# Routing and the first expert of a mixture layer: three groups of instructions in another order

## The chip, the cores and the metric

The kernel runs on one core of a Trainium2 chip. The metric is the device time of one launch in microseconds (us), the median of three runs. Beside the runs there is one profiled execution, whose trace gives the start and the length of each instruction on each engine: TensorE (PE, with its weight loads as PEld), VectorE (DVE), ScalarE (ACT), GpSimd (POOL) and SyncE (SP), which here only issues DMAs.

## The reference

Four layers on x of 8 x 256 rows of 512, each added to x: an attention with a decay mask, a feed-forward of ternary weights, an attention with gates (mLSTM), and a mixture of experts. The change lies at the border between the third and the fourth. The fourth is, cut to what matters:

```python
def _moe_core(x, gate_w, w13, w2):            # x: 2048 rows of 512, E = 32 experts, K = 4
    N = T * K
    C = 2 * N // E
    logits = jnp.einsum('th,eh->te', x, gate_w)
    scores = jax.nn.softmax(logits, axis=-1)
    topk_w, topk_ids = jax.lax.top_k(scores, K)
    topk_w = topk_w / jnp.sum(topk_w, axis=-1, keepdims=True)
    ...
    buf = jnp.zeros((E, C, x.shape[1]), x.dtype).at[sorted_eid, pos].set(x[tok], mode='drop')
    gu = jnp.einsum('ech,ehf->ecf', buf, w13)
    g, u = jnp.split(gu, 2, axis=-1)
    eo = jnp.einsum('eci,eih->ech', jax.nn.silu(g) * u, w2)
    out_slots = eo[sorted_eid, pos]
    return jnp.zeros_like(x).at[tok].add(out_slots * flat_w[order][:, None])

h = _rmsnorm(hidden_states, norm_w)
routed = _moe_core(x, gate_w, w13, w2)
shared = jax.nn.silu(x @ shared_gate_w) * (x @ shared_up_w) @ shared_down_w
out = residual + (routed + shared)
```

So each row goes through a shared expert and through the four experts of its own.

## The kernel before

**Stages.** Rows are kept as 16 tiles of 128, and, turned, as four chunks of 512 columns (`g.qT`). The first two layers and the gated attention take the first 520 us. Around 520 us the last normalized rows are turned, the logits are computed (`logits`, `logits_turned`), and `choices` finds each row's four experts, the rank of each expert by the number of its rows, and each row's place in its expert's list. `route` turns these into lists: which row stands in which slot of which rank (`g.tok_of`), and to which row a slot's result is added (`g.to`). Then the 32 experts run in the order of their ranks (`layer1_ffn`), from about 600 us to the end.

**The shared expert** fills TensorE beside all this. Its chunks 0 and 1 (`EARLY = 2`) are cut into pieces that `filler()` puts between the steps of the attention's last rounds and of `choices`. A piece is a pair: matmuls, and what follows on them (`rest`), which waits in the list `then` for the next call. For the last first-product piece of chunk 1, `rest` is `gated(1)`: a silu on ScalarE (L1068) and a product on VectorE (L1069) that gives `act`, which the second products (`down`, L1080) of chunk 1 read. Each `yield` of `choices` is one call of `filler()`. Up to here the order of TensorE, ScalarE, VectorE, GpSimd and SyncE is that of the program (`manual_schedule`).

Chunks 2 and 3 are done by `glu` and `down` in `layer1_ffn` (L1775 to L1781). `glu` writes four products of a chunk (pg and pu for two halves of the hidden width, L1744) into three PSUM buffers (`gu`), a silu frees the buffer of pg, the product L1749 on VectorE frees that of pu and gives `act`. `down` (L1761) has two buffers (`po`) and reads both halves of `act`; VectorE adds its result to the row (L1780) and SP writes the row out (L1781). A product of f32 shows in the trace as two instructions for each matmul of the code, so a chunk is 32 instructions of L1744 and 16 of L1761.

**Order in the free stretch.** From `route` to the last shared product no order is written out. The framework's scheduler makes it when the program is built: it steps through the program with its own estimates of durations, and gives each engine that falls free the first instruction in program order that is ready by these estimates. On the chip each engine then keeps that order, ready or not. `route` stands ahead of chunks 2 and 3 in the program, so its work goes first where it is ready, and the shared work fills in.

**The lists.** `route` builds them in eight passes (`n`, two for each of a row's four places). A pass compares the list numbers of eight row tiles with the numbers 0 to 127 of all lists (`to_list`, L1645, two buffers), and then for each tile makes a matrix of slot numbers (`to_slot`, L1651, four buffers) whose product with the tile's part of `to_list` is added up in one PSUM buffer (`pl`, L1654). So there are 64 slots and 64 list products. Ahead of the passes stand constants: three iotas on GpSimd (`iota`, `iop`, `lists_i`), their casts on VectorE, and the comparisons that give `g.is_rank` and `g.expert` (L1629 to L1637); `spare` is read only after the passes (L1666), `g.expert` by the load of an expert's weights on SP (L1724). After the passes: `tok_of` (L1663), and the check whether an expert has too many rows (`limit`, `g.over`; L1672 to L1682), which the code has last in `route`.

Before `route`, `layer1_ffn` fills a tile with zeros on GpSimd and writes it from GpSimd's queue to the 512 rows behind the output (L1768 to L1770), to which the empty slots add.

**The first expert.** `fetch` gathers a block of up to 128 rows from memory by `tok_of` (an indirect DMA on GpSimd's queue, six buffers). `turn_block(r, j)` turns block j of rank r: four transposes on TensorE (pt, L1801, two buffers), a product with the norm's weights on VectorE (xT, L1802), the slots' weights (`of`, L1796), and it issues the gather of block j of rank r + 2. From L1831 on the order of TensorE, ScalarE and VectorE is written out again; it begins with the four turns of rank 0.

```python
        with tc.manual_schedule(engines={E_.PE, E_.Activation, E_.DVE}):
            for j in range(NJ):
                turn_block(0, j)
            for r in range(E):
                w13, w2 = load_expert(r)
                act = glu(ps, w13[:, :, :FI], w13[:, :, FI:], xT.pop(r), SLOTS[r], partial(turn_block, r + 1))
```

## Time and profile before

| What | us |
|---|---|
| runs: median (lowest to highest) | 1031.09 (1029.36 to 1031.83) |
| the profiled execution | 1030.34 |
| its span in the trace | 1028.6 |
| last shared pieces of chunk 1 done (TensorE) | 547.2 |
| first list product | 554.6 |
| last list product | 582.6 |
| first gather issued on GpSimd | 584.3 |
| first turn of rank 0 | 595.95 |
| first product of rank 0 | 599.44 |

The times below the span are starts or ends in the trace, counted from the span's start. An engine's busy time in a window of the trace says how full it is there; the idle time that the trace notes in front of an instruction, with the instruction that ended it, says for what it waited.

### The profile page before, as it was taken

The page shows a single profiled execution, that of the slowest core. Times are in us where ns is not written, and L with a number is a line of the kernel's source. Part 1 is how long each engine was busy: PE and PEld are TensorE (multiplying, and loading weights), DVE is VectorE, ACT ScalarE, POOL GpSimd, SP SyncE. Part 2 cuts the span into 40 slices and gives each one's busy share as a digit, 9 for nine tenths or more (in the row PEclk, how much of TensorE's full clock was granted, in tenths as well). Part 3 has the DMA queues.
Part 4 walks back from the last instruction along what each step waited for, and adds up shares of the span by engine and source line. Part 5 has one row for each costly group of instructions (what it writes and reads, how often), then busy time and mean ns, then how long its engine had stood idle before and what let it go on. Part 6 is the DMA issues. An engine that isn't in the chain of part 4 may idle for free.

```text
span 1028.6 us, 14755 instructions
## 1 busy us (share of the span) xinstructions
PE 990.8 (96%) x5220; PEld 603.4 (59%) x5220; DVE 527.2 (51%) x1338; ACT 404.1 (39%) x693; POOL 404.5 (39%) x501
## 2 busy tenths in 40 slices
PE   8999999989999899999999999999999999999995
PEld 6766656534444356666544445555666666778783
DVE  7446566679987858878969831211212221122110
ACT  4443343457776757877430002122122222221221
POOL 0023443430111113788303225455455555444432
PEclk9999999999999999999999999999999999999998
DMA  9853333324332511231116248687788788889983
GB/s 344 294 185 117 141 118 130 103 67 76 60 58 40 92 39 45 64 126 55 62 62 225 82 147 189 169 209 190 182 207 207 207 210 231 220 242 240 230 225 46
DMA packets 101154, 152.67 MB, mean 148 GB/s; under 512 B 39592, under 2 KB 42280, under 8 KB 101036
## 3 DMA queue, kind: packets, MB, share of 16 engines
q1 hardware_dynamic: 82128, 107.04, 34.1%
q0 software_dynamic: 18944, 44.60, 19.4%
q8 instruction: 43, 0.70, 0.3%
q14 instruction: 39, 0.32, 0.1%
HBM read 110.42 MB, written 33.23 MB: 140 GB/s over the span
## 4 chain that ended last, share of the span: by engine, by line
PE 72%; DVE 13%; DMA 4%; POOL 4%; ACT 3%; issue 2%; SPq 0%; POOLq 0%; ACTq 0%; DVEq 0%
PE po L1761 14%; PE pg L1744 13%; PE pu L1744 13%; PE pw L399 5%; PE pz L435 5%; PE pt L1801 3%; PE p L1203 2%; DMA wst<-in_w1T 2%; DVE am L1220 2%; PE pgu L1060 2%; DVE h L1216 2%; DVE ct L844 2%; PE po L415 1%; PE po L412 1%; DVE st L127 1%
## 5 line engine op out<-in xcount | busy, mean ns | idle before, releaser
L1749 DVE TENSOR_TENSOR act<-pu,sg 128x264 f32<-128x264 f32 (+22 forms) x68 | 31.9, 469 | 313.5 <-PE pu L1744 303.2
L1786 POOL DMA_INDIRECT xg<-h_d,tok_of x85 | 83.6, 983 | 196.0 <-DVE of L1796 64.1
L1805 POOL DMA_INDIRECT out_x<-eo,to x85 | 132.9, 1564 | 55.1 <-ACT eo L1843 34.3
L1761 PE MATMUL po<-w,act 128*128 128x512 f32 (+10 forms) x456 | 143.1, 489 | 0.0
L1744 PE MATMUL pg<-xT,w 128*128 128x216 f32 (+21 forms) x512 | 134.9, 406 | 0.7 <-DVE xT L1802 0.7
L1843 ACT ACTIVATE eo<-po,slotw 128x512 f32<-128x512 f32 (+10 forms) x114 | 65.1, 576 | 173.9 <-PE po L1761 166.9
L1744 PE MATMUL pu<-xT,w 128*128 128x216 f32 (+21 forms) x512 | 133.3, 403 | 0.0
L1744 PEld LDWEIGHTS pg<-xT,w 128*128 128x128 f32 x512 | 93.2, 190 | 33.2 <-issue 16.9
L1748 ACT ACTIVATE sg<-pg 128x264 f32<-128x264 f32 (+22 forms) x68 | 28.5, 420 | 213.5 <-PE pg L1744 213.5
L1744 PEld LDWEIGHTS pu<-xT,w 128*128 128x128 f32 x512 | 96.8, 190 | 26.2 <-issue 5.6
L1203 PE MATMUL p<-wq,xqT 128*128 128x512 bf16 (+1 forms) x384 | 82.9, 367 | 6.4 <-DVE qi L1224 3.1
L1761 PEld LDWEIGHTS po<-w,act 128*128 128x128 f32 (+10 forms) x456 | 54.1, 155 | 57.5 <-issue 47.6
L420 POOL TENSOR_TENSOR y<-y,gam 128x512 f32<-128x512 f32 x16 | 20.2, 1265 | 135.5 <-DVE y L81 135.5
L1203 PEld LDWEIGHTS <-xqT 128*128 128x128 bf16 x384 | 37.6, 99 | 50.2 <-issue 13.6
L1802 DVE TENSOR_TENSOR xT<-pt,nw 128x512 f32<-128x512 f32 (+12 forms) x85 | 51.1, 601 | 20.5 <-PE pt L1801 20.5
L435 PE MATMUL pz<-wo,wyT 128*128 128x512 f32 x128 | 57.8, 594 | 0.7 <-ACT wyT L429 0.7
L399 PE MATMUL pw<-wg,xnT 128*128 128x512 f32 x128 | 57.8, 594 | 0.0
L1801 PEld LDWEIGHTS pt<-ident,xg 128*128 128x128 f32 (+15 forms) x340 | 39.1, 140 | 23.6 <-PE po L1761 10.5
L127 DVE BATCH_NORM_STATS2 st<-x 128x6 f32<-128x512 f32 x64 | 43.8, 687 | 9.2 <-POOL x L913 4.5
L1801 PE MATMUL pt<-ident,xg 128*128 128x128 f32 (+15 forms) x340 | 47.0, 260 | 0.6 <-DVE xT L1802 0.5
L844 DVE SCALAR_TENSOR_TENSOR ct<-pqk,xe 128x768 f32<-128x768 f32 x44 | 40.0, 951 | 8.8 <-PE pqk L840 8.1
L1211 ACT ACTIVATE sg<-p,s 128x512 f32<-128x512 f32 (+1 forms) x48 | 31.1, 648 | 28.2 <-PE p L1203 28.1
(338 smaller groups left out, 1678.7 us busy)
## 6 DMA issues: line engine op xcount, KB each, us to landing
w<-in_w SPq DMA_DIRECT2D x32, 1024.0 KB
w<-in_w SPq DMA_DIRECT2D x32, 512.0 KB
wst<-in_w1T SPq DMA_DIRECT2D x8, 704.0 KB
wst<-in_w3T SPq DMA_DIRECT2D x8, 704.0 KB
wst<-in_w2T SPq DMA_DIRECT2D x6, 768.0 KB
x<-in_x SPq DMA_DIRECT2D x16, 256.0 KB
ctxT<-in_ctxT_d SPq DMA_DIRECT2D x4, 1024.0 KB
raw<-in_ctx SPq DMA_DIRECT2D x16, 256.0 KB
```

What stands on the lines that cost most here:

```text
L127: first = g.nc.vector.bn_stats(st, x)
L399: nc.tensor.matmul(pw, lhsT=xnT[c][:, k, o : o + P], rhs=wg[:, k, :], start=k == 0, stop=k == KD - 1)
L435: nc.tensor.matmul(pz[i], lhsT=wyT[i][:, k, :], rhs=wo[:, k, :], start=k == 0, stop=k == KD - 1)
L844: nc.vector.scalar_tensor_tensor(ct[:, r : r + 2, :], pqk[:, :, : S + P], 1.0 / math.sqrt(HD1), xe[:, r : r + 2, :], ALU.mult, ALU.mult,)
L1203: nc.tensor.matmul(both[:, m, : z - a], lhsT=xqT[:, k, :], rhs=w[:, k, a:z], start=k == 0, stop=k == KD - 1)
L1744: nc.tensor.matmul(pp[:, :n], lhsT=w[:, k, cols], rhs=xT[:, k, :n], start=k == 0, stop=k == KD - 1)
L1761: nc.tensor.matmul(po[h * at : h * at + n, :cols], lhsT=act[:, m, j * P : j * P + n], rhs=w[:, m, h * cols : (h + 1) * cols], start=m == 0 ...
L1786: nc.gpsimd.indirect_dma_start(out=xg[:n], out_offset=None, in_=h_d, in_offset=bass.IndirectOffsetOnAxis(ap=g.tok_of[:n, r, j : j + 1], ax ...
L1801: nc.tensor.transpose(pt[:, k, :n], xg[:n, k * P : (k + 1) * P], g.ident[:n, :n])
L1802: nc.vector.tensor_mul(xT, pt[:, :, :n], g.nw.unsqueeze(2).to_broadcast([P, KD, n]))
L1805: return nc.gpsimd.indirect_dma_start(out=g.out, out_offset=bass.IndirectOffsetOnAxis(ap=rows, axis=0), in_=eo, in_offset=None, compute_op ...
L1843: nc.scalar.activation(eo[:n, at : at + cols], po, AF.Copy, scale=w[r][:n, j : j + 1])
```

## The change

Three places.

- `choices` yields once more, with `True`, between the counts' `order` and the comparisons that give the ranks. At that yield no piece of the shared expert is taken; what waits in `then`, which is `gated(1)` of chunk 1, is run.
- `zeros()` is called by `route` after the three iotas instead of by `layer1_ffn` ahead of them. The casts of `lists` and `slots` come ahead of that of `col`. `spare`, `g.is_rank` and `g.expert` are made after the first of the eight passes and not ahead of it.
- The two loops over chunks 2 and 3 come after `fetch`, `turn`, `add` and `turn_block` in the code, and the eight first gathers are issued ahead of them. The four turns of rank 0 stand ahead of the second products of the row tiles 14 and 15, outside the order that is written out.

```diff
--- before.py
+++ after.py
@@ -1171,8 +1171,12 @@
             lgT = logits()
             filler()
             logits_turned(lgT)
-            for _ in choices(g, work, ps):
-                filler()
+            for only_rest in choices(g, work, ps):
+                if not only_rest:
+                    filler()
+                elif then[0]:
+                    then[0]()
+                    then[0] = None
             while pieces or then:
                 filler()
 
@@ -1553,6 +1557,7 @@
         nc.tensor.matmul(pc, lhsT=onesb, rhs=mask[:, i, :], start=i == 0, stop=i == NT - 1)
     nc.vector.tensor_copy(count, pc)
     nc.vector.scalar_tensor_tensor(order, col, -1.0 / P, count, ALU.mult, ALU.add)
+    yield True
     nc.vector.tensor_tensor(
         sq, order.unsqueeze(1).to_broadcast(square), order.unsqueeze(2).to_broadcast(square), ALU.is_gt
     )
@@ -1587,7 +1592,7 @@
     yield
 
 
-def route(g, keep, pool, ps):
+def route(g, keep, pool, ps, zeros):
 
 
     nc = g.nc
@@ -1604,38 +1609,22 @@
 
     lists_i = new("lists_i", [P, E, NJ], I32)
     nc.gpsimd.iota(lists_i, pattern=[[16, E], [1, NJ]], base=0, channel_multiplier=0)
+    zeros()
     slots_of = new("slots_of", [P, E])
     for r in range(E):
         if r == 0 or SLOTS[r] != SLOTS[r - 1]:
             nc.gpsimd.memset(slots_of[:, r:], float(SLOTS[r]))
+    lists = new("lists", [P, E * NJ], F16)
+    nc.vector.tensor_copy(lists, lists_i.rearrange("p e j -> p (e j)"))
+    slots = new("slots", [P, P], F16)
+    nc.vector.tensor_copy(slots, iota)
     col = new("col", [P, E])
     nc.vector.tensor_copy(col, iota[:, :E])
-
-    slots = new("slots", [P, P], F16)
-    nc.vector.tensor_copy(slots, iota)
-    lists = new("lists", [P, E * NJ], F16)
-    nc.vector.tensor_copy(lists, lists_i.rearrange("p e j -> p (e j)"))
     row = new("row", [P, 1])
     nc.vector.tensor_copy(row, iop)
     number = new("number", [P, NT])
     nc.vector.tensor_scalar(number, col[:, :NT], float(P), 1.0, ALU.mult, ALU.add)
     nc.vector.tensor_scalar(number, number, row, None, ALU.add)
-    spare = new("spare", [P, NJ])
-    nc.vector.tensor_scalar(spare, col[:, :NJ], float(P), float(T + 1), ALU.mult, ALU.add)
-    nc.vector.tensor_scalar(spare, spare, row, None, ALU.add)
-
-
-    g.is_rank = new("is_rank", square, pool=keep)
-    nc.vector.tensor_tensor(
-        g.is_rank, rank.unsqueeze(1).to_broadcast(square), col.unsqueeze(2).to_broadcast(square), ALU.is_equal
-    )
-    sq = new("sq", square)
-    nc.vector.tensor_mul(sq, g.is_rank, col.unsqueeze(1).to_broadcast(square))
-    at = new("at", [P, E])
-    nc.vector.tensor_reduce(at, sq, AX.X, ALU.add)
-    g.expert = new("expert", [P, E], I32, keep)
-    nc.vector.tensor_copy(g.expert, at)
-
 
     pl = ps.tile([P, E, NJ], F32, tag="rt", name="pl", bufs=1)
     half = NT // 2
@@ -1655,6 +1644,22 @@
                 pl.rearrange("p e j -> p (e j)"), lhsT=to_slot, rhs=to_list[:, i - i0, :],
                 start=n == 0 and i == 0, stop=n == 2 * TOPK - 1 and i == NT - 1,
             )
+        if n == 0:
+            spare = new("spare", [P, NJ])
+            nc.vector.tensor_scalar(spare, col[:, :NJ], float(P), float(T + 1), ALU.mult, ALU.add)
+            nc.vector.tensor_scalar(spare, spare, row, None, ALU.add)
+
+
+            g.is_rank = new("is_rank", square, pool=keep)
+            nc.vector.tensor_tensor(
+                g.is_rank, rank.unsqueeze(1).to_broadcast(square), col.unsqueeze(2).to_broadcast(square), ALU.is_equal
+            )
+            sq = new("sq", square)
+            nc.vector.tensor_mul(sq, g.is_rank, col.unsqueeze(1).to_broadcast(square))
+            at = new("at", [P, E])
+            nc.vector.tensor_reduce(at, sq, AX.X, ALU.add)
+            g.expert = new("expert", [P, E], I32, keep)
+            nc.vector.tensor_copy(g.expert, at)
 
 
     plf = new("plf", [P, E, NJ])
@@ -1765,21 +1770,16 @@
             return [po[h * at : h * at + n, :cols] for h in range(parts)]
 
         zero = work.tile([P, D], F32, tag="eo", name="zero", bufs=3)
-        nc.gpsimd.memset(zero, 0.0)
-        for j in range(NJ):
-            nc.gpsimd.dma_start(out=g.out[T + j * P : T + (j + 1) * P, :], in_=zero)
+
+        def zeros():
+            nc.gpsimd.memset(zero, 0.0)
+            for j in range(NJ):
+                nc.gpsimd.dma_start(out=g.out[T + j * P : T + (j + 1) * P, :], in_=zero)
+
         sg_w, su_w, sd_w = g.shared
         ps = ctx.enter_context(tc.tile_pool(name="f1ps", bufs=2, space=PSUM, reuse_waits="tile"))
         with tc.tile_pool(name="f1rwork", bufs=1, reuse_waits="tile") as rwork:
-            route(g, rp, rwork, ps)
-        for c in range(EARLY, NCH):
-            act = glu(ps, sg_w, su_w, g.qT[c])
-            for j in range(CH // P):
-                i = c * (CH // P) + j
-                (po,) = down(ps, act, sd_w, j)
-                nc.vector.tensor_add(g.X[i], po, g.X[i])
-                nc.sync.dma_start(out=g.out[i * P : (i + 1) * P, :], in_=g.X[i])
-
+            route(g, rp, rwork, ps, zeros)
         def fetch(r, j, n=P):
 
             xg = work.tile([P, D + E], F32, tag="xg", name="xg", bufs=6)
@@ -1826,11 +1826,20 @@
             if r + 2 < E and j < len(BLOCKS[r + 2]):
                 xg[r + 2].append(fetch(r + 2, j, BLOCKS[r + 2][j]))
 
+        for c in range(EARLY, NCH):
+            act = glu(ps, sg_w, su_w, g.qT[c])
+            for j in range(CH // P):
+                i = c * (CH // P) + j
+                if i == NT - 2:
+                    for first in range(NJ):
+                        turn_block(0, first)
+                (po,) = down(ps, act, sd_w, j)
+                nc.vector.tensor_add(g.X[i], po, g.X[i])
+                nc.sync.dma_start(out=g.out[i * P : (i + 1) * P, :], in_=g.X[i])
+
         before = []
         E_ = mybir.EngineType
         with tc.manual_schedule(engines={E_.PE, E_.Activation, E_.DVE}):
-            for j in range(NJ):
-                turn_block(0, j)
             for r in range(E):
                 w13, w2 = load_expert(r)
                 act = glu(ps, w13[:, :, :FI], w13[:, :, FI:], xT.pop(r), SLOTS[r], partial(turn_block, r + 1))
```

## The prediction

> **What bounds the kernel now.** I read the page's head first, then the chain of waits, then the waits, the windows and the timelines of each engine around the edit.
>
> ```profile
> span 1028.6 us, 14755 instructions
> PE 990.8 (96%) x5220; PEld 603.4 (59%) x5220; DVE 527.2 (51%) x1338; ACT 404.1 (39%) x693; POOL 404.5 (39%) x501
> PE 72%; DVE 13%; DMA 4%; POOL 4%; ACT 3%; issue 2%; SPq 0%; POOLq 0%; ACTq 0%; DVEq 0%
> ```
>
> TensorE is busy 96% of the span, so an edit that shortens nothing it computes can win back only its waits near the edit. From 537 to 600 us, the stretch that the diff touches, these are all of them (line, who was waited for, us in total, times, longest):
>
> ```profile
> PE po L1080 <- DVE act L1069: 1.4, 1, 1.4
> PE pl L1654 <- DVE to_slot L1651: 1.2, 1, 1.2
> PE pg L1744 <- DVE xT L1802: 0.7, 1, 0.7
> PE pt L1801 <- DVE xT L1802: 0.5, 1, 0.5
> ```
>
> One for each third of the change: 3.8 us in all. The windows say what stands beside them (start:end, length, then busy time of PE, PEld, DVE, ACT, POOL, granted clock, DMA share, GB/s):
>
> ```profile
> 537.00:541.00 4.00, 2.72 (x18) 1.43 (x16) 3.85 (x7) 0.00 (x0) 0.59 (x1) 1.00 0.00 0
> 547.00:553.00 6.00, 6.00 (x15) 2.47 (x13) 5.97 (x14) 0.60 (x1) 3.94 (x26) 1.00 0.97 351
> 560.00:567.00 7.00, 7.00 (x30) 3.35 (x30) 7.00 (x20) 0.60 (x1) 0.00 (x0) 1.00 0.59 223
> 574.00:583.00 9.00, 9.00 (x41) 4.38 (x40) 8.96 (x29) 0.00 (x0) 0.00 (x0) 1.00 0.10 39
> 596.00:600.00 4.00, 2.70 (x19) 1.87 (x18) 3.23 (x11) 0.00 (x0) 2.27 (x3) 1.00 0.60 198
> ```
>
> See VectorE: 3.85 of 4, 5.97 of 6, 7.00 of 7. From 537.2 to 583 us it has no idle, beside a TensorE that is full too. There are two rails, and an edit that moves work about on VectorE's rail without removing any doesn't move that rail's end. Three lines of the timelines matter (start, us, engine):
>
> ```profile
> 557.82 1.95 DVE L1672 TENSOR_TENSOR sq<-is_rank,slots_of 128x1024 f32<-128x1024 f32 x1
> 566.75 0.69 DVE L1749 TENSOR_TENSOR act<-pu,sg 128x512 f32<-128x512 f32 x1
> 582.75 1.94 PE L1761 MATMUL po<-sw,act 128*128 128x512 f32 x4
> ```
>
> The first two are work of low priority that got a place among the slots: VectorE takes it when a slot must wait for its buffer, that is, when TensorE sits in a shared product. The third is what TensorE does after the last list product (582.64).
>
> **Part 1, gated rows first.** VectorE now does is_gt (1.24), the reduction (1.23) and a small one (0.04, with 0.13 of gaps) before act L1069, which runs 540.36 to 541.05. Put after L1555, which ends at 537.65, act ends near 538.36; its inputs are there, since the last pgu ends at 536.34 and sg starts at 536.36 for 0.60, to 536.96. TensorE's second products (L1080) wait 1.39 us for it and then wait no more. Behind act on VectorE stands the ranks' chain, 0.69 later, and then as before: the sum up to 541.05 is the same. Gain on TensorE's rail: 1.39, so shared chunk 2 starts at 545.83 and not at 547.22. On VectorE's rail: 0.
>
> **Part 2, numbers before zeros, ranks behind the first lists.** On POOL's queue iop (0.15) and lists_i (0.52) go ahead of the memset (0.55) and the four zero issues (2.18). lists_i is ready by about 546 instead of 548.3; the zeros issue under 1 us later, and nobody reads those rows before the first adds at 616.7. The 22 memsets of slots_of still end near 552.2 and are first read at 557.82. The cast of lists (0.14) had no wait in front of it, so this alone is worth 0. What counts is the move: is_rank 1.14, sq 1.23, at 1.13, expert 0.08, spare 0.07 + 0.13 = 3.78 us go behind the first eight slots. The first slot, ready at 554.55, is then ready at 550.77, and the 1.21 us in which TensorE waits for it can go. The 3.78 come back between list 0 and list 1, so list 1 starts at 555.79 as before. SP's first expert load hangs on expert: 553.97 becomes some 2.9 us (a list of 1.13 and eight slots of 0.22) later. Its product starts at 599.44, and the DMA share is already 0.00 in 567 to 574, so some 30 us cover it; without that cover those 2.9 would be the price.
>
> **Part 3, turning early.** Now 595.95 (first pt) to 599.44 (first pg) is 3.49 us, of which four turns of 0.44 are work: 1.74 of waiting, in idle gaps and stretched pt. The turns go ahead of the last two second products, 8 instructions or 3.43 us, which hide the xT chain (three of 0.60 and one of 0.41). Of the eight gathers that the code has ahead, six go out at once; the first starts at 584.27 and lands at 588.75 (4.5 later), the next three start at 585.69, 586.97, 588.22, so by the same row they land near 590.2, 591.5 and 592.7. TensorE reaches the place after the sixth product at 588.82 + 3.43 = 592.25 (less what parts 1 and 2 win). All but the last block have then landed, and a product stands between. Bounds: -1.74, and about -0.1 if TensorE comes 2.6 early and waits 1.6 for the fourth block with nothing between. I take -1.74. Queued behind the turns are the last adds L1780 and their row writes on SP, which nothing near waits for; POOL's gathers 7 to 10 (from 596.82) start earlier. [...]
>
> **The sum.** Parts 1 and 2 would give 1.39 + 1.21 = 2.60 only if TensorE did six more shared instructions (0.43 each) ahead of the last list product, which VectorE's rail holds at 582.3. Before, 66 of the 96 shared instructions are done by then and 30 remain: 582.75 to 595.95. Count at the start of list 1, 555.79: before, 16 done. After, from 545.83, 9.96 us less 8 list products of 0.06 is room for 22. But the order in this stretch is worked out ahead by the scheduler, and its clock had VectorE 1.2 us too fast just here (that is the 1.21 wait). The trace can't show the new order. If it errs as much again, TensorE stands 1.2 to 1.5 us before the first slot and has 18 done, 2 more. Bounds 0 and 6 instructions, 0 to 2.60 us; the nearest row is that same wait, so I take 2, or 0.86. Sum: 0.86 + 1.74 = 2.60. The profiled execution took 1030.34 (span 1028.6 and 1.74 around it) and becomes 1027.7. The median of the runs, 1031.09, is 0.75 above it: 1031.09 - 2.60 = **1028.5**.
>
> **Rivals.**
> A, everything kept: 2.60 + 1.74 = 4.34, so 1026.8. For it: TensorE's groups between 556 and 582 hold 50 shared instructions and 56 list products, 21.5 + 3.4 of 26.4 us, so there is 1.5 us of slack to fit more in. Against it: VectorE full to 583.
> B, slower: the shared products run out. Without any act of its own TensorE can do 48 instructions: chunk 2's 32 first products and 16 of chunk 3, as three buffers allow. Act L1749 has the lowest priority and comes only at a break in the slots; before, it came at 566.75, when 38 were spent, 10 in reserve. With six more spent the reserve is 4, one group. If act misses one break more, TensorE runs dry, slots never wait for a buffer, and so no break comes at all: VectorE runs the 37 slots left at 566.64 (0.223 each) and four lists (1.13) to 579.4, and only then act. After it 48 instructions, 20.6 us, and the turns, 1.76, follow act's 0.6 and 0.2 of handing over: 602.6 against 599.44, so 3.2 slower, 1034.3; if it runs dry with 40 spent, 3.4 more. It decides from the point where act comes after the 48th shared instruction. Against it: the four in reserve, and the low work at 557.82 that takes the earlier breaks as before.
> In B TensorE works 8 list products (0.5 us) per 2.9 us of VectorE, and here the clock stayed at 1.00 through a window with 2.72 of 4 busy. [...]
> C, the edit doesn't do what it says: the turns still end up behind the last product, and parts 1 and 2 drown in VectorE's rail: 0, so 1031.1. For it: that order is the scheduler's. Against it: the turns come first in the program, and the first gather lands 3.5 us before the place.
>
> **How the numbers follow.** Forecast 0.38, A 0.25, B 0.33, C 0.04. The range: A's 1026.8 with 0.4 for the spread of runs, to B's 1034.3 with 0.7 for part of its tail: 1026.4 to 1035.0; beyond it lies B's dry case at 40 and little else. The forecast's own range is 1027.4 to 1029.8. What a measurement of this kernel can tell is about 0.3%, 3.1 us: the forecast is beyond it in about a third of its chance (0.13), A in nine tenths (0.23): faster 0.36. B is beyond it, its price being a lower end, in nine tenths (0.30): slower 0.30. The rest, 0.34, is the same.
>
> **What would show it.** Right: no wait at L1080 for act L1069, no idle between pt, xT and the first expert pg, and that pg at about 596.8; VectorE still without idle to 583, the last list product within a microsecond of 582.6, 28 shared instructions after it. A: 24 after it, first pg at 595.1. B: the first act L1749 behind the last slot, near 579.4, TensorE idle by several us between 565 and 580, first pg near 602.6. Wrong altogether: a change of more than a microsecond after the first expert, where the diff orders nothing anew.

## The result and the profile after

The changed kernel takes 1033.51 us (median of eight runs, 1031.54 to 1036.59), the kernel before, run beside it, 1029.87 (eight runs, 1027.96 to 1031.83). The ratio is 1.0039, 95% interval 1.0027 to 1.0051: 0.4% slower, where a gain of 2.6 us was forecast. The profiled execution took 1034.76, its span 1033.0 against 1028.6. Lines have shifted: slots are L1640, list products L1643, shared first products L1749, act L1754, second products L1766, slot weights `of` L1796, turns L1801.

The page's busy times, in the first line below, show little of it: TensorE 992.3 us against 990.8. The waits of TensorE between 529 and 612 us show more (line, who was waited for, us in total, times, longest):

```profile
PE 992.3 (96%) x5220; PEld 604.4 (59%) x5220; DVE 528.0 (51%) x1338; ACT 403.8 (39%) x693; POOL 405.0 (39%) x501
PE pl L1643 <- DVE to_slot L1640: 3.3, 1, 3.3
PE po L1766 <- DVE act L1754: 3.0, 2, 2.6
```

Of the four waits shown before, those for act L1069 and the two for xT are gone; the one for the first slot has grown from 1.21 to 3.26, and a new one, of 2.56, stands at the shared expert's second products. The timeline of TensorE has both (start, us, engine, line; in brackets the idle time before and who ended it):

```profile
539.17 7.11 PE L1080 MATMUL po<-sw,act 128*128 128x512 f32 x16
546.12 3.60 PE L1749 MATMUL pg<-qT,sw 128*128 128x512 f32 x8
552.98 0.45 PE L1643 MATMUL pl<-to_list,to_slot 128*128 128x128 f16 x2 [3.26 <-DVE to_slot L1640]
...
554.40 3.63 PE L1749 MATMUL pu<-qT,sw 128*128 128x512 f32 x4
...
584.97 0.22 PE L1643 MATMUL pl<-to_list,to_slot 128*128 128x128 f16 x1
...
594.67 4.54 PE L1766 MATMUL po<-sw,act 128*128 128x512 f32 x6 [2.56 <-DVE act L1754]
599.04 1.04 PE L1801 MATMUL pt<-ident,xg 128*128 128x128 f32 x8
...
604.14 3.28 PE L1749 MATMUL pg<-xT,w 128*128 128x464 f32 x8
```

See four things. The second products of chunk 1 (first row) run without a wait, as part 1 meant. Only eight shared instructions stand between them and the first list product; before the change there were fourteen. Four instructions of L1749 take 3.63 us at 554.40 where four took 1.94 before, and six of L1766 take 4.54 where six take 2.78. And the first expert's product has no wait in front of it, but starts at 604.14.

Why work is slower just after these two waits, the windows of one microsecond tell (start:end, length, busy time of PE, PEld, DVE, ACT, POOL, then the granted clock):

```profile
554.00:555.00 1.00, 1.00 (x6) 0.59 (x5) 1.00 (x2) 0.00 (x0) 0.00 (x0) 0.74 0.07 16
555.00:556.00 1.00, 1.00 (x2) 0.34 (x1) 1.00 (x4) 0.00 (x0) 0.00 (x0) 0.50 0.00 0
556.00:557.00 1.00, 1.00 (x3) 0.35 (x2) 1.00 (x2) 0.00 (x0) 0.00 (x0) 0.50 0.00 0
557.00:558.00 1.00, 1.00 (x5) 0.30 (x3) 1.00 (x3) 0.00 (x0) 0.00 (x0) 0.56 0.00 0
...
595.00:596.00 1.00, 1.00 (x3) 0.37 (x2) 0.00 (x0) 0.00 (x0) 0.00 (x0) 0.72 0.53 204
596.00:597.00 1.00, 1.00 (x3) 0.48 (x2) 0.69 (x1) 0.00 (x0) 0.00 (x0) 0.50 0.00 0
597.00:598.00 1.00, 1.00 (x2) 0.34 (x2) 0.00 (x0) 0.00 (x0) 0.00 (x0) 0.50 0.38 143
598.00:600.00 2.00, 2.00 (x11) 1.18 (x10) 0.75 (x2) 0.00 (x0) 0.08 (x1) 0.79 0.16 59
```

Before, the clock was 1.00 throughout this stretch. Now it falls to 0.50 1.5 us after the end of the first wait and 0.8 us after that of the second. Worked out from these rows, at half speed were 0.52 + 1 + 1 + 0.88 = 3.4 us the first time and 0.56 + 1 + 1 + 0.84 = 3.4 the second; half of that, 1.7 us of work each time, is lost.

**Where the time went.** I measure from the start of the count products (pc) to the first expert's first product, since the two profiles already differ by 0.55 us ahead of that: 63.10 before, 67.25 after, 4.15 more (the spans: 4.4 more). The waits were 1.39 + 1.21 + 0.51 + 0.74 = 3.85 and are 3.26 + 0.44 + 2.56 = 6.26: 2.41 more. Half speed adds two times 1.7, or 3.4. Against it stand about 1.5 us, an estimate, in which TensorE was held up before without being idle in the record: list products that came one by one as their slots did (groups of 0.68, 0.90 and 0.62 us, where 0.3 to 0.4 is usual) and stretched turns. That makes 4.3, of 4.15 measured.

**What VectorE did meanwhile.** Its timeline at both places (rows that read an accumulator, 0.08 us each, are left out):

```profile
549.93 1.21 DVE L1634 TENSOR_TENSOR to_list<-lists,lg 128x1024 f16<-128x1024 f16 x1
551.06 0.17 DVE L1626 TENSOR_SCALAR number<-col 128x16 f32<-128x16 f32 x1
551.14 0.19 DVE L1649 TENSOR_SCALAR spare<-col 128x4 f32<-128x4 f32 x1
551.21 1.22 DVE L1654 TENSOR_TENSOR is_rank<-lg,col 128x1024 f32<-128x1024 f32 x1
552.35 0.22 DVE L1627 TENSOR_SCALAR number<-number,row 128x16 f32<-128x16 f32 x1
552.48 0.22 DVE L1650 TENSOR_SCALAR spare<-spare,row 128x4 f32<-128x4 f32 x1
552.61 1.42 DVE L1640 TENSOR_SCALAR to_slot<-slots,lg,number 128x128 f16<-128x128 f16 x6
...
590.43 0.19 DVE L1796 SCALAR_TENSOR_TENSOR of<-xg,is_rank 128x32 f32<-128x32 f32 x1 [3.08 <-DMA xg<-h_d,tok_of]
592.50 0.23 DVE L1796 SCALAR_TENSOR_TENSOR of<-xg,is_rank 128x32 f32<-128x32 f32 x1 [1.87 <-DMA xg<-h_d,tok_of]
593.81 0.19 DVE L1796 SCALAR_TENSOR_TENSOR of<-xg,is_rank 128x32 f32<-128x32 f32 x1 [1.07 <-DMA xg<-h_d,tok_of]
593.93 0.69 DVE L1754 TENSOR_TENSOR act<-pu,sg 128x512 f32<-128x512 f32 x1
```

Above: the comparisons of the ranks, which the code has behind the first eight slots, run ahead of all slots. `number` takes two instructions and the second reads the first; between them the scheduler put what it found ready, and is_rank is 1.22 us long. Every slot reads `number`. Below: the slots' weights `of` of rank 0, each of which needs a gathered block, stand on VectorE ahead of act of chunk 3. The product that act reads had ended at 591.1; act came at 593.93, behind the third gather.

The profile before has the first of the four `of` in this place already:

```profile
588.75 0.19 DVE L1796 SCALAR_TENSOR_TENSOR of<-xg,is_rank 128x32 f32<-128x32 f32 x1 [3.13 <-DMA xg<-h_d,tok_of]
...
589.09 0.69 DVE L1749 TENSOR_TENSOR act<-pu,sg 128x512 f32<-128x512 f32 x1
```

There it held up nothing, since the product that act reads ended only at 588.98. But the row from which the prediction reads that the first gather lands at 588.75 is this `of`, and the next piece of work behind it on VectorE is the act for which TensorE waits after the change.

### The profile page after: what moved, and what is told of

Same layout as the page of the kernel before. It is cut to its first block, busy times and chain, and to the rows that moved or that the text cites. A ratio compares the mean times of both kernels' runs of the same rounds, so it can differ in the third digit from the quotient of the medians.

```text
span 1033.0 us, 14751 instructions
## 1 busy us (share of the span) xinstructions
PE 992.3 (96%) x5220; PEld 604.4 (59%) x5220; DVE 528.0 (51%) x1338; ACT 403.8 (39%) x693; POOL 405.0 (39%) x501
## 4 chain that ended last, share of the span: by engine, by line
PE 69%; DVE 14%; DMA 5%; POOL 4%; ACT 3%; issue 3%; POOLq 0%; SPq 0%; DVEq 0%; ACTq 0%
PE po L1766 14%; PE pu L1749 13%; PE pg L1749 12%; PE pw L399 5%; PE pz L435 5%; PE pt L1801 3%; PE p L1207 2%; DMA wst<-in_w1T 2%; DVE am L1224 2%; DVE h L1220 2%; PE pgu L1060 2%; DVE ct L844 2%; DVE st L127 1%; PE po L415 1%; PE po L412 1%
## 5 line engine op out<-in xcount | busy, mean ns | idle before, releaser
L1754 DVE TENSOR_TENSOR act<-pu,sg 128x264 f32<-128x264 f32 (+22 forms) x68 | 31.9, 469 | 312.2 <-PE pu L1749 312.2
L1766 PE MATMUL po<-w,act 128*128 128x512 f32 (+10 forms) x456 | 143.1, 489 | 0.0
L1749 PE MATMUL pg<-xT,w 128*128 128x216 f32 (+21 forms) x512 | 134.8, 406 | 0.0
L1749 PE MATMUL pu<-xT,w 128*128 128x216 f32 (+21 forms) x512 | 133.3, 403 | 0.0
L1749 PEld LDWEIGHTS pg<-xT,w 128*128 128x128 f32 x512 | 93.3, 190 | 32.8 <-issue 17.3
L1749 PEld LDWEIGHTS pu<-xT,w 128*128 128x128 f32 x512 | 96.8, 190 | 26.2 <-issue 5.6
L1766 PEld LDWEIGHTS po<-w,act 128*128 128x128 f32 (+10 forms) x456 | 54.1, 155 | 57.4 <-issue 47.9
L1801 PEld LDWEIGHTS pt<-ident,xg 128*128 128x128 f32 (+15 forms) x340 | 39.3, 140 | 23.5 <-PE po L1766 10.5
L1801 PE MATMUL pt<-ident,xg 128*128 128x128 f32 (+15 forms) x340 | 46.8, 260 | 0.0
```

What stands on the lines that cost most here:

```text
L1749: nc.tensor.matmul(pp[:, :n], lhsT=w[:, k, cols], rhs=xT[:, k, :n], start=k == 0, stop=k == KD - 1)
L1766: nc.tensor.matmul(po[h * at : h * at + n, :cols], lhsT=act[:, m, j * P : j * P + n], rhs=w[:, m, h * cols : (h + 1) * cols], start=m == 0 ...
L1801: nc.tensor.transpose(pt[:, k, :n], xg[:n, k * P : (k + 1) * P], g.ident[:n, :n])
```

## The experiments

Theory 1: part 2's order makes the first slot late against a TensorE that arrives sooner; theory 2: the slot weights of part 3 hold act back; theory 3: a wait of this length costs its own length and 1.7 us more, by the clock. The recorded expectations call the three together theory Q. The rival is the prediction's B, shared products that run dry before act. Here all twelve runs in one table: the median, the ratio to the kernel before, run beside it, with its interval, and from each profile the times from the counts to the first list product and to the first expert's first product, TensorE's waits in the stretch, and whether the clock fell to 0.50 there. The last four columns describe one execution of each kernel; whether the clock fell in its other executions is not shown (last section).

| Kernel | us | ratio | list | expert | waits | clock fell (one execution) |
|---|---|---|---|---|---|---|
| before | 1029.38 to 1029.87 | 1 | 18.26 | 63.10 | 1.39, 1.21, 0.74, 0.51 | no |
| after | 1033.51 | 1.0039 (1.0027–1.0051) | 16.09 | 67.25 | 3.26, 0.44, 2.56 | twice |
| part1_alone | 1029.70 | 1.0006 (0.9995–1.0016) | 17.82 | 62.90 | 2.42, 0.7, 0.5 | no |
| part2_alone | 1030.35 | 1.0009 (0.9998–1.0020) | 16.30 | 64.08 | 1.39, 1.83, 0.5, 0.7, 0.5 | no |
| part3_alone | 1030.63 | 1.0011 (0.9997–1.0025) | 18.25 | 63.64 | 1.38, 1.20, 2.43 | no |
| parts1and2 | 1031.16 | 1.0020 (1.0008–1.0032) | 16.08 | 64.79 | 3.26, 0.4, 0.7, 0.5 | once |
| weights_held | 1028.76 | 0.9993 (0.9981–1.0005) | 16.08 | 62.99 | 3.26, 0.47 | once |
| numbers_first | 1028.63 | 0.9996 (0.9985–1.0008) | 14.75 | 62.75 | 2.79, 0.45 | once |
| ranks_last | 1026.83 | 0.9975 (0.9965–0.9985) | 14.75 | 62.28 | 2.79 | once |
| slots_unbroken | 1040.58 | 1.0105 (1.0091–1.0119) | 16.09 | 74.61 | 3.27, five later of 0.2 to 1.1 | twice, once for 14 us |
| wait_refilled | 1032.75 | 1.0030 (1.0020–1.0039) | 16.31 | 65.83 | 2.48 | once |
| wait_covered | 1028.24 | 0.9989 (0.9978–1.0000) | 16.30 | 62.39 | 2.48 | once |
| ranks_last_covered | 1024.96 | 0.9951 (0.9937–0.9965) | 15.45 | 58.25 | 0.24 | no |
| ranks_last_covered_more | 1024.83 | 0.9948 (0.9934–0.9961) | 16.31 | 58.45 | 0.79 | no |

### The three parts by themselves

Each is the kernel before with one part of the change: the extra `yield True` of `choices`; zeros, casts and the block of ranks in `route`; the loops over chunks 2 and 3 with the early turns. A fourth has the first two. part2_alone and parts1and2 also have the loops over chunks 2 and 3 behind `turn_block` and the first gathers ahead of them, as the kernel after has, with the turns of rank 0 left where they were; what that move does by itself was not separated. The core of each:

```diff
     nc.vector.scalar_tensor_tensor(order, col, -1.0 / P, count, ALU.mult, ALU.add)
+    yield True
```

```diff
+        if n == 0:
...
+            g.is_rank = new("is_rank", square, pool=keep)
```

```diff
+                if i == NT - 2:
+                    for first in range(NJ):
+                        turn_block(0, first)
                 (po,) = down(ps, act, sd_w, j)
```

> Before with the last gated piece of chunk 1 ahead of the ranks' comparisons, nothing else. TensorE gets to chunk 2 about 1.4 us earlier and has 14 shared instructions ahead of the first list product, whose slot is as late as before or 0.2 later: its wait there grows from 1.2 to about 2.6 us. Theory Q: the gain of 1.4 turns into that wait and the end stays within 0.5 us; if the wait halves the clock, 1.7 slower. Rival R: 0.4 to 1.4 us faster.

> Before with the routing's order changed (numbers ahead of zeros, ranks behind the first pass), nothing else. Theory Q: is_rank gets in ahead of the second half of number, which all slots wait for; the first slot comes at about 552.0 and not at 550.8; TensorE has only 8 shared instructions ahead of the first list product and stands from 550.7, a wait of 1.5 to 2 us, short enough that the clock stays at 1.00: last list product and end within 1 us of before, 0 to 1.0 us slower. Rival R: the wait is gone or stays at 1.2, 0 to 1.2 us faster.

> Before with the turns of rank 0 moved ahead of the last two second products, nothing else. Theory Q (VectorE's queue is held): three of the slot weights (of, L1788 here) stand on VectorE ahead of the second act of chunk 3, and each waits for its gather; act starts near 591.9 and not at 589.1, TensorE waits about 2.5 us for it, and after a wait that long its clock is halved for some 3.4 us, 1.7 us more; less the 1.74 that the turns hide: first product of rank 0 near 602, 2 to 2.5 us slower than before. Rival R (the two rails): the queue doesn't matter, the turns hide as forecast, 1.7 us faster.

> The changed kernel with the turns of rank 0 back at the head of the written order. Theory Q: TensorE waits 3.3 us for the first slot as in the changed kernel, the clock is halved for about 3.4 us behind it, and the turns cost 3.5 us again: 1.5 to 2.5 us slower than before. Rival R (the loss is all of part 3): within 1 us of before or faster.

**Part 1 alone** removes its wait of 1.39, and the wait for the first slot becomes 2.42, exactly 1.21 longer: 0.2 of the 1.39 is kept. **Part 2 alone** has its lists 2 us sooner and yet a longer wait for them, 1.83, since the built order now has eight shared instructions ahead of the first list product and not fourteen. **Part 3 alone** wins the 1.25 us of waits at the turns and pays 2.43 at act; 2 to 2.5 us more than before were expected, with the clock at half speed, but in the profiled execution the clock stayed at 1.00 and the stretch is only 0.54 longer:

```profile
587.90 0.19 DVE L1788 SCALAR_TENSOR_TENSOR of<-xg,is_rank 128x32 f32<-128x32 f32 x1 [1.93 <-DMA xg<-h_d,tok_of]
588.85 0.19 DVE L1788 SCALAR_TENSOR_TENSOR of<-xg,is_rank 128x32 f32<-128x32 f32 x1 [0.74 <-DMA xg<-h_d,tok_of]
588.96 0.69 DVE L1749 TENSOR_TENSOR act<-pu,sg 128x512 f32<-128x512 f32 x1
```

Here too (VectorE of part3_alone) act starts as the third `of` ends. No part alone differs from before beyond its interval. **Parts 1 and 2 together** do, by 0.2%: the 1.39 and the 1.83 of part 2 alone are here one wait of 3.26, and behind it the clock falls; 1.4 us of waiting saved by part 1 plus a list begun 2 us sooner end in a stretch 1.7 us longer than before. So the parts aren't a sum of their prices: two waits behind which the clock stayed at 1.00 (part2_alone) became one behind which it fell (0.50 in each microsecond from 552 to 555).

### The slot weights held back

```diff
-            turn(..., w[r][:, j : j + 1])
+            turn(..., w[r][:, j : j + 1] if weigh else None)
...
-                        turn_block(0, first)
+                        turn_block(0, first, False)
...
+            for j, n in enumerate(BLOCKS[0]):
+                tc.add_manual_dep(weight(xg[0][j], n, 0, w[0][:, j : j + 1]).ins, added.ins.name, NoSync)
```

The kernel after, with the four slot weights of rank 0 behind the shared expert's last add (`added`; `NoSync` sets an order on the engine and adds no wait), where they are still far ahead of their first use.

> The changed kernel, with the four slot weights (of) of rank 0 held on VectorE behind the shared expert's last add; the turns stay early. Theory Q (in-order waits on VectorE, then a halved clock): the 2.6 us wait of TensorE for the second act of chunk 3 and the 1.7 us of halved clock behind it go, the 1.7 us that the turns hide stay; from the count products (pc) to the first product of rank 0 some 63.0 us (changed kernel 67.25, before 63.10): within 1 us of before, 4 faster than the changed kernel. Rival R (turning early costs by itself, by the gathers or the adds): 1 us or less faster than the changed kernel.

TensorE then does eight second products without a wait (first row, from its timeline), since VectorE does act as soon as the product that it reads is done (second row, from VectorE's):

```profile
589.33 3.86 PE L1766 MATMUL po<-sw,act 128*128 128x512 f32 x8
589.60 0.69 DVE L1754 TENSOR_TENSOR act<-pu,sg 128x512 f32<-128x512 f32 x1 [4.00 <-PE pu L1749]
```

The stretch falls from 67.25 to 62.99, 4.26 us: 2.56 of wait and 1.76 of half-speed work (4.54 against 2.78). Theory 2 holds, and this one order is as large as the difference between the kernel after and the kernel before: with it undone the ratio is 0.9993, level with before. What the rest of the change wins elsewhere the first wait of 3.26, still there, eats up.

### The first slot

`numbers_first` is weights_held with `col`, `row` and `number` ahead of `lists` and `slots`, so that the second half of `number` is never held up. `ranks_last` adds to it that the whole block from is_rank to the check for too many rows stands behind `to`, after the lists. `slots_unbroken` is weights_held with is_rank ordered behind the last slot of the first pass, as the change's own code reads.

```diff
-            g.is_rank = new("is_rank", square, pool=keep)
-            nc.vector.tensor_tensor(
...
-    nc.vector.scalar_tensor_tensor(g.to, plf, 1.0, free, ALU.subtract, ALU.add)
+    listed = nc.vector.scalar_tensor_tensor(g.to, plf, 1.0, free, ALU.subtract, ALU.add)
+    g.is_rank = new("is_rank", square, pool=keep)
+    ranked = nc.vector.tensor_tensor(
...
+    tc.add_manual_dep(ranked.ins, listed.ins.name, NoSync)
```

(The lines are those of `ranks_last`; `slots_unbroken` has the same dependence on the pass's last `to_slot` and leaves the block where it is.)

> weights_held, and in route col, row and number are made ahead of lists and slots, so that nothing stands between list 0 and the first slots. Theory Q: the first slot comes 1.3 to 1.8 us earlier; TensorE waits about 2.4 us for it and not 3.3, and the clock stays at 1.00 in most runs; pc to first product 61 to 62 us: 1 to 2 us faster than before. Rival V (VectorE's rail alone sets the end; when the first slot comes doesn't matter): as weights_held, within 0.5 us of it.

> numbers_first, and the ranks' comparisons, experts and the check for too many rows (about 7 us of VectorE) are held behind the lists. Theory V2 (two rails: VectorE's work ahead of tok_of sets the last list product): last list product about 7 us earlier, 40 shared instructions behind it, TensorE full from the first slot on; pc to first product 58 to 59.5 us: 3.5 to 5 us faster than before. Rival: VectorE's rail isn't the limit, or the experts' weights, which are now asked for near 580, come late: 2 us faster or less.

> weights_held, and the ranks' comparison may not go ahead of the last slot of the first pass (an order on VectorE, no wait). In the order that follows the act of chunk 2 misses its break: TensorE has done all 48 shared instructions that need no act, and the last 33 list products stand with nothing between. This is rival B of the prediction made on purpose: last list product near 580, first act near 580, first product of rank 0 about 3.2 us later than before, more if the clock is halved in between: 3 to 6 us slower than before. If B's price is wrong (TensorE's idle time is made up elsewhere): within 1 us.

With numbers first the list starts 14.75 us after the counts instead of 16.08, by the 1.22 of is_rank; but the built order answers with six shared instructions ahead of it instead of eight, so that the wait shrinks by 0.47 only, and the clock still falls (0.50 in 552 to 554). 1 to 2 us faster than before was expected; there is no gain beyond the interval, over before or over weights_held. Ranks last frees VectorE's rail: the last list product comes 42.4 us after the counts (578.3 less 535.9) instead of the 48.3 of weights_held, all later waits are gone, and the kernel is 0.25% faster than before. I had expected more; what was missing is in one row of the table, the first wait of 2.79 and the clock after it (0.50 in 552 to 554).

Slots unbroken is rival B in full. Slots that follow one another without a break keep act off VectorE until the lists are done, and TensorE has nothing but list products (VectorE's timeline, then windows):

```profile
578.20 1.87 DVE L1640 TENSOR_SCALAR to_slot<-slots,lg,number 128x128 f16<-128x128 f16 x8
579.99 0.18 DVE L1687 TENSOR_TENSOR past<-lg,limit 128x32 f32<-128x32 f32 x1
580.09 0.68 DVE L1759 TENSOR_TENSOR act<-pu,sg 128x512 f32<-128x512 f32 x1
```

```profile
568.00:572.00 4.00, 3.38 (x16) 1.33 (x14) 4.00 (x12) 0.00 (x0) 0.00 (x0) 0.99 0.10 38
572.00:576.00 4.00, 2.21 (x10) 1.04 (x10) 4.00 (x14) 0.00 (x0) 0.00 (x0) 0.50 0.00 0
576.00:580.00 4.00, 2.93 (x14) 1.35 (x13) 4.00 (x16) 0.00 (x0) 0.00 (x0) 0.50 0.00 0
580.00:584.00 4.00, 3.59 (x6) 1.62 (x7) 2.58 (x12) 0.60 (x1) 2.06 (x2) 0.50 0.14 30
584.00:588.00 4.00, 4.00 (x8) 1.54 (x7) 1.38 (x2) 0.00 (x0) 2.84 (x4) 0.80 0.77 214
```

Act comes at 580.09 (the prediction's B had it at 579.4 for the slots' end), and the first expert's product at 609.44. No single idle gap in these windows is longer than 1.12 us, yet the clock is at 0.50 for some 13.6 us, while VectorE hands out one list product of 0.06 us at a time. Against weights_held the stretch is 11.6 us longer, the time 11.8.

### Filling the wait, or computing something useful in it

The last four kernels aim at the first wait alone. `wait_refilled` is weights_held with four matmuls more (eight instructions, 3.44 us) into pu's buffer ahead of the first list product, whose sums are thrown away. `wait_covered` puts the first list product of weights_held behind sixteen instructions of the first products instead of eight; `ranks_last_covered` that of ranks_last behind fourteen instead of six, `ranks_last_covered_more` behind sixteen. Only the order on TensorE is set (`ahead` is the first list product):

```diff
-                        nc.tensor.matmul(
+                        made = nc.tensor.matmul(
                             pp[:, :n], lhsT=w[:, k, cols], rhs=xT[:, k, :n], start=k == 0, stop=k == KD - 1
                         )
+                        if ahead is not None and m == 0 and pp is pu and k == 3:
+                            tc.add_manual_dep(ahead.ins, made.ins.name, NoSync)
```

That is sixteen; k == 2 gives fourteen. In `wait_refilled` this stands in front of the loop over k instead:

```diff
+                    if ahead is not None and m == 0 and pp is pu:
+                        for again in range(4):
+                            made = nc.tensor.matmul(pp[:, :n], lhsT=w[:, 0, cols], rhs=xT[:, 0, :n], start=True, stop=True)
+                        tc.add_manual_dep(ahead.ins, made.ins.name, NoSync)
```

> weights_held with four more products of the second half of the first block of columns (eight instructions of 0.43 us, their sums thrown away by the real ones that start the group anew), put ahead of the first list product, so that TensorE computes through the wait of 3.26 us. If the granted clock falls because TensorE stands still: the wait falls from 3.26 to under 0.3, the clock stays at 1.00 in every 1 us window from 551 to 560, the first list product still starts some 16 us after the counts (weights_held: 535.12 to 551.20), and the stretch from the counts to the first expert's first product shrinks by the half-speed loss alone, some 1.5, from 62.99 to about 61.5; the median goes from 1028.8 to 1027.0-1028.2. If the clock falls for another reason (the mass of work on the other engines, the start of the list products): 0.50 is still granted for some 3 us after the first list product and the stretch stays at 62.5-63.2.

> weights_held with the first list product put behind the sixteenth instruction of the shared expert's first products rather than behind the eighth: no work added, only the order on TensorE. If TensorE is the bound there: wait 3.26 gone, clock 1.00, stretch from 62.99 to 58-59, median about 1024.5. If VectorE's slots are the second rail close behind (they run from 551 to 583 with 0.9 us of idle time): the last list product stays at 582-584, TensorE has fewer than 30 shared instructions left after it, and a wait for the first gathered rows or for act comes back; stretch 60-62, median 1026.5-1028.

> ranks_last with the first list product put behind fourteen instead of six instructions of the first products. In ranks_last TensorE had no wait but the first of 2.79 us, with a clock of 0.50 after it. Expected: that wait under 0.4, clock 1.00 throughout, stretch from the counts to the first expert's first product 62.28 less 2.79 less about 1.6 = 57.9 (before the edit 63.10), median 1022.5-1024, ratio about 0.994. If the waits only move on: a new one of 2-3 us at act or at the gathered rows, stretch 60-62, ratio 0.996-0.998.

> As ranks_last_covered, with sixteen instructions ahead of the first list product. The list then starts about 0.9 us later than it could; TensorE loses nothing by it as long as the rows come in time (30 shared instructions left after the last list product in ranks_last). Expected within 0.1% of ranks_last_covered; slower than it by 0.5-1 us if the lists set the end there.

The first two were misses, and alike: the wait ahead of the first list product is gone, and 2.48 us of it stand ahead of the fifth. TensorE and VectorE of wait_covered:

```profile
549.60 3.70 PE L1751 MATMUL pu<-qT,sw 128*128 128x512 f32 x8
553.13 0.69 PE L1643 MATMUL pl<-to_list,to_slot 128*128 128x128 f16 x4
553.66 1.08 PE L1751 MATMUL pg<-qT,sw 128*128 128x512 f32 x2
557.22 0.90 PE L1643 MATMUL pl<-to_list,to_slot 128*128 128x128 f16 x4 [2.48 <-DVE to_slot L1640]
557.95 3.16 PE L1751 MATMUL pg<-qT,sw 128*128 128x512 f32 x4
```

```profile
552.56 0.98 DVE L1640 TENSOR_SCALAR to_slot<-slots,lg,number 128x128 f16<-128x128 f16 x4
553.45 1.22 DVE L1660 TENSOR_TENSOR sq<-is_rank,col 128x1024 f32<-128x1024 f32 x1
554.59 1.22 DVE L1634 TENSOR_TENSOR to_list<-lists,lg 128x1024 f16<-128x1024 f16 x1
555.72 1.21 DVE L1662 TENSOR_REDUCE at<-sq 128x32 f32<-128x1024 f32 x1
556.85 0.97 DVE L1640 TENSOR_SCALAR to_slot<-slots,lg,number 128x128 f16<-128x128 f16 x4
```

Four slots fill the four buffers; the scheduler then gives VectorE the long comparisons, and TensorE, which has used up the four at once, waits for the next. So the wait comes from the 3.4 us of comparisons that VectorE does between the fourth slot and the fifth, two of them the ranks' (sq, at) and one the next list's, and not from TensorE's order alone. But the pair is a clean test of whether the fall follows the wait, as theory 3 has it: at the place of the old wait the clock now stays at 1.00, and after the new wait of 2.48 it falls (0.63 granted as the mean of 558 to 560; L1751 above, 3.16 instead of 1.94). Here the fall went where the wait went; the load on the other engines and the start of the list products stayed where they were. In wait_refilled the 3.44 us of useless work cost 2.84 in the stretch.

Where the ranks' block is away as well, the cover works. TensorE of ranks_last_covered_more:

```profile
548.34 3.70 PE L1755 MATMUL pu<-qT,sw 128*128 128x512 f32 x8
551.88 0.39 PE L1643 MATMUL pl<-to_list,to_slot 128*128 128x128 f16 x4
552.10 1.08 PE L1755 MATMUL pg<-qT,sw 128*128 128x512 f32 x2
...
594.02 3.28 PE L1755 MATMUL pg<-xT,w 128*128 128x464 f32 x8
```

There is no wait until 587, then one of 0.79 for act, and no half speed in the whole stretch (1.00 in every window from 535 to 600), which takes 58.45 us. ranks_last_covered gives 58.25 (57.9 expected). By their medians, 1024.83 and 1024.96, both are 0.5% faster than the kernel before: versions that beat both kernels, with all three parts of the change in them and three orders added (slot weights, ranks, first list product).

## Why the prediction was wrong

The time, 1033.51, lies inside the range, on the other side of the time before from the forecast. That it lies near rival B's 1034.3 is chance: what B describes did not happen.

- **Part 1, as written.** Act ends at 538.8, the second products run on without a wait, and VectorE's rail moves little (part1_alone: last list product done 47.2 us after the counts, before 46.6). The bound of 0 for parts 1 and 2 together, which the text names, is what part 1 alone shows (0.2 kept).
- **Part 2, the step that failed first:** "The first slot, ready at 554.55, is then ready at 550.77, and the 1.21 us in which TensorE waits for it can go." The first list product came 1.7 us later than that (16.09 after the counts, where 550.77 less 536.34 is 14.43), 1.3 of it because the block that I had moved "behind the first eight slots" is so moved in the code only; its first member ran between the halves of `number`. numbers_first, without that, comes to 14.75.
- **Its sequel in the sum,** "TensorE stands 1.2 to 1.5 us before the first slot and has 18 done, 2 more", took the wait of before as the measure of the scheduler's error. At the same point, 556.3 in the profile after, TensorE had 12 done: the built order put fewer shared instructions ahead of the list, the sooner it thought the list ready. The wait was 3.26. In numbers_first, where the slot is on time, it is still 2.79; so this step, and not is_rank, is the larger error. The step's lower bound, 0, excluded a loss, and no reason given there did. The lists end 48.3 us after the counts instead of 46.6, with 30 shared instructions behind them as before, where 28 were forecast.
- **Part 3, the step that failed worst.** "Queued behind the turns are the last adds" left out what `turn_block` itself puts on VectorE: the four `of`, the first three of which stood *ahead* of act of chunk 3. The gathers came as forecast: they let `of` go 5.2, 7.3 and 8.6 us after the last list product, where the text's 588.75, 590.2 and 591.5 are 5.8, 7.3 and 8.6 after 582.9. TensorE's turns were indeed hidden. What wasn't looked at was who else waits for a landed block: an in-order engine with urgent work behind it. Its price is 4.26 us, and undoing it alone brings the kernel level with before.
- **The clock** fell twice, at a cost of 3.4 of the 4.15 us, and the sum has nothing for it: the prediction reads only that it stayed at 1.00 through a window with 2.72 of 4 us busy. The profile before has two falls to 0.50 ahead of this stretch, from 220.22 and 360.16 us, behind waits of 2.52 and 1.55 us, each 3.41 us long. In the stretches of the table it fell behind waits of 2.48 to 3.27 us, and in slots_unbroken a second time around gaps of up to 1.12 us (last section).
- **Rival B** was not what happened (the first act L1754 came at 570.67, and 30 shared instructions were left after the last list product), but it was a true danger: slots_unbroken, where the code's order is enforced, has it. Its price, 3.2, was too low: 11.6. For 10 us TensorE had little but list products, and the second products after them ran partly at half speed (sixteen in 9.68 us instead of 7.11).

## What to carry to other kernels

When an edit lets work start earlier, list everything that the moved call issues on *every* in-order queue, and ask of each what it waits for and what urgent work stands behind it: here a side product that nobody needed soon held up one that TensorE needed at once. Where a scheduler makes the order, moving a block in the code doesn't move it on the engine, and making a producer sooner may only make its consumer wait sooner; read the built order, or fix the two or three instructions that matter. Several short waits can be cheaper than one wait of about their sum: here the clock stayed at 1.00 behind the 1.39 and the 1.83 of part2_alone and fell to 0.50 behind the 3.26 of parts1and2, whose stretch is 0.71 us longer. So place independent work between them.

## What the runs showed of the hardware

**When the clock fell.** Between the first matmul and the last, the trace of the kernel before has a granted clock of 0.50 twice, from 220.22 and 360.16 us, and that of the kernel after four times, from 219.97, 359.92, 554.48 and 595.43 us. Each of the six lasts 3.41 us and at half speed costs an estimated 1.7 us of work. The starts lie 139.95 us apart in the kernel before, and 139.95, 194.56 and 40.96 us in the kernel after, which is 41, 57 and 12 times 3.413. In the stretch of the edit they lie 1.5 and 0.8 us *after* work has begun again (552.98 and 594.67), and in wait_refilled 1.7 us after it (556.22; the mean clock is 1.00 up to 557, 0.97 in 557 to 558, then 0.50), so that the cost shows in the work and not in the wait.

**The length of a wait does not decide it.** In the stretch of the edit the clock stayed at 1.00 after waits of up to 2.43 us (part1_alone 2.42, part3_alone 2.43) and fell after those of 2.48 us (wait_refilled, wait_covered) to 3.27 us (slots_unbroken). But in the kernel before it stayed at 1.00 after a wait of 1.70 us that ends at 352.36 and fell after one of 1.55 us that ends at 357.89; in the kernel after, two waits of 1.70 us end at 352.69 and 358.37, and it fell after the second alone (in both with one of 0.53 between wait and fall). Nor do these two traces show it by the idle time of TensorE in the 3.413 us just ahead of a fall. That is 2.52 and 1.67 us before, and 2.32, 2.23, 1.92 and 2.56 us after; of the other stretches of this length, counted on from the falls, the idlest has 1.70 us before and 1.76 after, and the clock stayed at 1.00 behind it. What decides is not shown.

**One execution each.** So the "no" of part1_alone and part3_alone in the table holds for one execution. The twelve executions of part1_alone have mean clocks of 0.992 to 0.995, and the profiled one is the fastest of them, with 0.995; the eleven of part3_alone have 0.991 to 0.996, the profiled one 0.996. Half speed for 3.41 us takes 0.0017 off a mean over 1030 us, an estimate from these numbers; so in some of the others the clock most likely fell once or twice more. Where is not shown, as only one execution of each kernel has a trace.

**Half speed with short gaps.** In slots_unbroken the clock was at 0.50 for some 13.6 us around gaps of up to 1.12 us, with TensorE at work in 5.14 of the 8 us from 572 to 580 by the record; in the 4 us before that, at work in 3.38, it had 0.99. What such list products of 0.06 us count for is open.
